# Layer 0 of a four-layer image network: the Fourier products in quarters of TensorE's array, and the w_out products written some rounds later

## The chip, the cores and the metric

The kernel runs on one core of a Trainium2 chip. The metric is the device time in microseconds of one execution. The engines are TensorE (PE: matmuls; PEld: its weight loads), VectorE (DVE), ScalarE (ACT), GpSimd (POOL) and SyncE (SP, which only issues DMAs here). TensorE's clock is granted by a throttle, and the profile shows what was granted (1.00 is full speed).

## What is computed

Four layers, each x = x + layer(group_norm(x)), on x of shape 4 x 48 x 256 x 256 in float32. Layers 1 and 2 scan over rows and columns, layer 3 is a relative of layer 0. The change is in layer 0:

```python
h = jnp.einsum('bchw,oc->bohw', x, w_in)            # 48 -> 192 channels
h = depthwise_3x3(h, w_dw)
x1, x2 = jnp.split(h, 2, axis=1)
h = gelu(x1) * x2                                   # 96 channels
y = jnp.einsum('bchw,oc->bohw', h, w_out)           # 96 -> 48 channels
yp = y cut into 8 x 8 patches
f = jnp.fft.rfft2(yp) * fft_w                       # a weight per channel and wave
y = jnp.fft.irfft2(f, s=(8, 8)), patches put together again
```

The transform of an 8 x 8 patch is a product with a fixed 64 x 64 matrix (64 real waves), and so is its inverse.

## The kernel before

**Tiling.** Layer 0 works on pairs of images: 2 x 48 channels on the partitions. A pair is cut into 32 strips of 8 rows, so there are 64 strips. Before layer 0, `input_stats` reads x once for the group norm; layer 0 gathers the statistics (`bn_stats`, L432) that the norm ahead of layer 1 needs, so layer 1 starts when the last strip is done.

**One strip.** The steps, with the functions and lines of the kernel before:

- `fetch` and `normed` (L234, ACT): load rows, scale and shift them.
- `hidden` (L256, PE, then a copy L259 on ACT) and `hidden_rest` (L264, PE, then two copies L268 on DVE): w_in. The hidden channels are split: 64 of each half go to tiles `main`, the other 32 to `rest`.
- `lane` (L285, PE): the 3x3 taps on `main`, as products with diagonal 32 x 32 weights on 16 tiles of the array. Two lanes, l = 0 and 1, each do nine taps per image, 8 products a tap; a "round" is one tap of both lanes, 16 products. At the end of an image lane 0 does the gelu (L296, ACT, tile `gl`) and lane 1 the product with it (L299, DVE, tile `g`).
- `unit` (L314 ACT, L320 DVE, 16 half-taps a strip; L328 to L330 ACT; L334 DVE): the 3x3 taps on `rest`, on VectorE, and their gate `gr`.
- `mixed` (L355 from `gr`, L362 from `g`, PE): w_out, into two PSUM tiles `py`, copied to `y` by ACT (L368).
- `turned` (L379, PE): 16 transposes, 8 into each of two PSUM tiles `pt`, each copied to `yt` by ACT (L383).
- `waves` (L393, PE): 4 products of the 128 x 128 matrix `dft` (two patches at once, block diagonal) with 448 columns; four VectorE products with the mask (L399) make `z`.
- `back` (L415, PE): 16 products, z as weights of 128 x 96, the permuted inverse as 128 columns; 16 VectorE sums with the residual `res` (L426), 4 statistics (L432), and a store issued by POOL (L435).

In the profile each float32 product is two TensorE passes (two LDWEIGHTS and two MATMUL records).

**Order.** For PE, DVE and ACT the order of instructions is that in which the program issues them. `in_turns` writes it: in each turn both lanes issue a tap, then the pieces of `work` (the steps above, with a cost each) as far as a credit goes that grows by `pace` a tap, then the half-taps of `unit` for VectorE. A piece has a condition; `mixed` waits until the strip's six parts are counted in `taken`. The pieces come one after the other: w_out of the strip before, then the halo, w_in `rest`, the transposes, w_in `main`, `waves`, `back`. Lane 1 begins four turns after lane 0.

**PSUM.** Layer 0 has four PSUM buffers of two banks (pool `ps0`, 4 buffers), shared by all of `ph`, `pd`, `py`, `pt`, `pf` and `po`. Each lane holds one for nine taps; it is free when the gelu (lane 0) or the product g (lane 1) has read it. So a new tile waits for the engine that reads the old one.

The loop that orders the pieces, as it stands before:

```python
if n:
    yield (
        lambda: taken.get(n - 1, 0) == 6, 4.0, lambda: state.update(y=mixed(n - 1)),
    )
...
if n:
    yield always, 3.3, lambda: state.update(z=waves(state["yt"])), 2.2
...
self.in_turns([lane(0), lane(1)], work(), 0.57, self.aside([unit(n) for n in range(len(strips))]))
```

Of the kernel before, what the change touches and what calls it, by code (L numbers as in the profile page):

```python
# [17 lines left out]
C = 48  # L18
CC = 2 * C
NT = 5  # L20
# [10 lines left out]
class Net:  # L31
# [9 lines left out]
    def __init__(self, ctx, tc, args, out, B, H, W):  # L41
# [20 lines left out]
        self.dft = self.load("dft", [128, 128])  # L62
# [3 lines left out]
        self.idft_p = self.load("idft_p", [128, 128])  # L66
# [10 lines left out]
    def new_stats(self, halves=False):  # L77


        n = self.B if halves else self.NP  # L80
        t = self.stat.tile([CC, n, self.NP * self.NCH // n, 6], F32, name=f"st{n}", tag="st")
        return [t[:, p] for p in range(n)]

    def norm(self, stats):

        nc, n = self.nc, len(stats)
        grp = self.grp if n == self.NP else self.grp6
        with self.tc.tile_pool(name="ps_n", bufs=1, space=PSUM) as psn:
            t = self.stat.tile([CC, 8, n], F32, name="nrm", tag=f"nrm{n}")
            mv = self.stat.tile([CC, n, 2], F32, name="mv", tag=f"mv{n}")  # L90
            sc = self.stat.tile([CC, n, 2], F32, name="sc", tag=f"sc{n}")
# [3 lines left out]
            pm = psn.tile([CC, n], F32, name="pm")  # L95
# [5 lines left out]
            pv = psn.tile([CC, n], F32, name="pv")  # L101
# [13 lines left out]
    def by_image(self, scs):  # L115

        found = []
        for p in range(self.NP):
            for b in range(2):
                t = self.stat.tile([CC, 2], F32, name=f"si{p}{b}", tag=f"si{p}{b}")  # L120
                for k in range(2):
                    self.nc.sync.dma_start(t[k * C : (k + 1) * C, :], scs[p][b * C : (b + 1) * C, :])
                found.append(t)
        return found
# [21 lines left out]
    def layer0(self, scs, stats):  # L146
# [7 lines left out]
        with ExitStack() as st:  # L154
# [42 lines left out]
            mask = wp.tile([128, 1, 1, C], F32, name="mask")  # L197
            nc.vector.tensor_copy(mask[:, 0, 0, :], pm[:, 0, 0, 0:C])
# [3 lines left out]
            raws, mains, rests, scp = [], [], [], []  # L202
            for k in range(2):
                raws.append(wp.tile([128, RB + 1, W], F32, name=f"raw{k}", tag=f"raw{k}"))
# [142 lines left out]
            def mixed(n):  # L347

                g, gr = state.pop((n, "g")), state.pop((n, "gr"))
                y = mid.tile([112, NQ, RB, PW], F32, name="y", tag="y", bufs=1)  # L350
# [15 lines left out]
                for k, py in enumerate(pys):  # L366
                    r = 2 * R2 * k
                    nc.scalar.copy(  # L368
                        y[:, :, r : r + 2 * R2, :].rearrange("p q r w -> p r q w"),
                        py[0:112].rearrange("p j r (q w) -> p (j r) q w", w=PW),  # L370
# [3 lines left out]
            def turned(y):  # L374
                yt = mid.tile([128, NQ, 112], F32, name="yt", tag="yt", bufs=1)
                for q0 in range(0, NQ, 8):
                    pt = ps.tile([128, 2, MM], F32, name="pt", tag="w")
                    for q in range(8):
                        nc.tensor.transpose(  # L379
                            pt[:, q // 4, q % 4 * 112 : (q % 4 + 1) * 112],  # L380
                            y[:, q0 + q].rearrange("p r w -> p (r w)"), self.ident[0:112, 0:112],
# [6 lines left out]
            def waves(yt):  # L388
                z = mid.tile([128, NQ, 2, C], F32, name="z", tag="z", bufs=1)
                for q0 in range(0, NQ, 8):  # L390
                    pf = ps.tile([128, 2, MM], F32, name="pf", tag="w")
                    for k in range(2):
                        nc.tensor.matmul(  # L393
                            pf[:, k, 0 : 4 * 112], self.dft,
                            yt[:, q0 + 4 * k : q0 + 4 * k + 4, :].rearrange("p q c -> p (q c)"),
                            start=True, stop=True,
                        )
                    for b in range(2):
                        nc.vector.tensor_tensor(  # L399
                            z[:, q0 : q0 + 8, b, :].rearrange("p (k q) c -> p k q c", k=2),  # L400
                            pf[:, :, 0 : 4 * 112].rearrange("p k (q c) -> p k q c", q=4)[:, :, :, 64 * b : 64 * b + C],
                            mask.to_broadcast([128, 2, 4, C]), ALU.mult,
                        )
                return z

            def back(n, z):

                p, h0 = strips[n]
                res = io.tile([CC, RB, W], F32, name="res")
                nc.sync.dma_start(res, self.x0[p, :, h0 : h0 + RB, :])  # L410
                xo = io.tile([CC, 2, self.WB, 2, RH, 2, 8], F32, name="xo")
# [933 lines left out]
```

## Time and profile before

| | |
|---|---|
| median of 3 runs | 14288.26 us (14286.5 to 14288.58) |
| the profiled execution's own time | 14286.4 us |
| its span, first to last instruction | 14284.6 us |
| mean granted TensorE clock over the span | 0.962 |
| busy: PE, DVE, ACT, POOL | 13196.5, 7393.2, 3661.9, 1340.3 us |
| layer 0, from the first to the 64th strip's w_out | 299.1 to 3277.7 us |
| PE busy, DVE busy, granted clock in that stretch | 2786.26, 2207.80 us, 0.94 |
| L415: busy, mean of a pass, passes | 239.1 us, 275 ns, 2048 |
| L393: busy, mean of a pass, passes | 210.7 us, 555 ns, 512 |
| L355: idle time ahead of it | 126.8 us, all of it ended by g (L299) |
| L379: idle time ahead of it | 56.6 us, of it 38.7 ended by ACT's gl and 15.8 by DVE's rest |

How to read it: a line of a group gives line, engine, operation, out<-in by the program's names, shapes and count, then busy time and mean duration of one, then the engine's idle time just ahead of them and what ended it. Passes on different tiles of the array overlap, so a mean duration is longer than the time that a pass adds. A line of the timeline gives start, duration, engine, line, operation and count, and in brackets the idle time ahead and what ended it. A line of stretches gives the stretch and its length, busy time and count of PE, PEld, DVE, ACT and POOL, then the granted clock, the DMA share and GB/s.

### The profile page before, as it was taken

Reading aid. Unit: us, or ns where it says so; the run is one execution under the profiler, and the core shown is the slowest. Engines: PE = TensorE matmul, PEld = TensorE weight load, DVE = VectorE, ACT = ScalarE, POOL = GpSimd, SP = SyncE. Lnnn points to the kernel's source line nnn. Section 1 sums busy time; section 2 is a strip of 40 time slices with the busy share of each in tenths; the row PEclk is TensorE's granted clock in tenths of the full one; section 3 lists DMA queues with packets and bytes.
Section 4 is the critical chain, followed back from the end, with each engine's and each line's share of the span. In section 5 each row is a group of like instructions: output and inputs, shape, how many; then the busy total and the mean of one; then the engine's idle time right before and its main releaser. Section 6 shows DMA issues by size and latency. Waiting matters only on the chain.

```text
span 14284.6 us, 338560 instructions
## 1 busy us (share of the span) xinstructions
PE 13196.5 (92%) x155716; PEld 8194.6 (57%) x155716; DVE 7393.2 (52%) x12064; ACT 3661.9 (26%) x3558; POOL 1340.3 (9%) x974
## 2 busy tenths in 40 slices
PE   2999999998999898889998988799999999999999
PEld 1444443446777676667776766555555555555555
DVE  6777777773333334443333344555555555455555
ACT  1333333332233000012230000133333333333333
POOL 0000010000000004410000044200000000000000
PEclk9999999999999999899999998899999999999999
DMA  7222222216755876777558767311111111111110
GB/s 166 49 54 48 55 51 52 50 48 119 152 139 153 161 146 166 179 146 151 135 160 159 154 149 192 75 24 20 24 20 24 20 24 20 20 24 20 21 23 18
DMA packets 1168858, 1219.07 MB, mean 85 GB/s; under 512 B 1026004, under 2 KB 1030604, under 8 KB 1106572
## 3 DMA queue, kind: packets, MB, share of 16 engines
q1 hardware_dynamic: 1069324, 649.62, 23.2%
q0 software_dynamic: 87488, 445.55, 11.2%
q10 hardware_dynamic: 10624, 102.24, 3.5%
q8 instruction: 1222, 20.02, 0.6%
q14 instruction: 200, 1.64, 0.0%
HBM read 699.84 MB, written 497.42 MB: 84 GB/s over the span
## 4 chain that ended last, share of the span: by engine, by line
PE 76%; DVE 10%; DMA 6%; ACT 3%; issue 2%; SPq 1%; POOL 1%; ACTq 0%; DVEq 0%; POOLq 0%
PE acc L609 33%; PE pd L1010 9%; PE pp L993 8%; PE pd L285 5%; PE pd L1026 4%; PE pz L964 4%; DMA blk<-x 3%; DVE acc L320 3%; PE po L1106 2%; PE pf L953 2%; PE ph L264 2%; PE ph L256 2%; DMA x<-blk 2%; PE py L355 1%; PE pf L393 1%
## 5 line engine op out<-in xcount | busy, mean ns | idle before, releaser
L609 PE MATMUL acc<-line,w_down 96*96 96x256 f32 x12240 | 2650.7, 379 | 42.5 <-DMA in<-x 23.5
L609 PEld LDWEIGHTS acc<-line,w_down 96*96 96x96 f32 x12240 | 1996.0, 163 | 696.6 <-issue 43.2
L1010 PE MATMUL pd<-z_a,diag 32*32 32x512 f32 x37152 | 1692.0, 596 | 2.7 <-ACT xt L943 0.7
L1070 DVE SCALAR_TENSOR_TENSOR acc<-z_b,wd,acc 128x1024 f32<-128x1024 f32 (+1 forms) x1056 | 1329.2, 1260 | 626.0 <-ACT acc L1067 595.4
L609 PE MATMUL acc<-line,w_left 96*96 96x256 f32 x6120 | 1362.3, 386 | 247.8 <-DVE line L792 247.8
L609 PE MATMUL acc<-line,w_right 96*96 96x256 f32 x6120 | 1338.0, 381 | 100.3 <-DVE line L753 36.2
L993 PEld LDWEIGHTS pp<-c_idft,z 128*128 128x128 f32 x10240 | 1185.0, 184 | 339.8 <-issue 195.4
L609 PEld LDWEIGHTS acc<-line,w_left 96*96 96x96 f32 x6120 | 1016.7, 166 | 593.1 <-DVE line L792 253.8
L285 PE MATMUL pd<-main,diag 32*32 32x512 f32 x36864 | 1338.4, 602 | 6.5 <-DVE g L299 6.4
L320 DVE SCALAR_TENSOR_TENSOR acc<-rest,wd,acc 128x1024 f32<-128x1024 f32 x1024 | 1326.7, 1341 | 1.9
L993 PE MATMUL pp<-c_idft,z 128*128 128x128 f32 x10240 | 1255.2, 282 | 65.6 <-DVE g_b L1037 39.0
L609 PEld LDWEIGHTS acc<-line,w_right 96*96 96x96 f32 x6120 | 1003.9, 164 | 434.5 <-DVE line L753 38.4
L1026 PE MATMUL pd<-z_b,diag 32*32 32x512 f32 x18432 | 1001.5, 602 | 59.2 <-DVE g_a L1053 39.6
L966 DVE TENSOR_TENSOR z<-pz,mask 128x512 f32<-128x512 f32 x1024 | 702.8, 686 | 519.1 <-PE pz L964 515.5
L753 DVE SCALAR_TENSOR_TENSOR line<-acc,b_right,in 96x256 f32<-96x256 f32 x1020 | 489.4, 480 | 880.6 <-PE acc L609 836.9
L285 PEld LDWEIGHTS pd<-main,diag 32*32 32x32 f32 x36864 | 525.8, 103 | 685.3 <-issue 514.4
L1010 PEld LDWEIGHTS pd<-z_a,diag 32*32 32x32 f32 x37152 | 601.6, 103 | 538.5 <-issue 358.8
L672 DVE TENSOR_TENSOR line<-acc,in 96x256 f32<-96x256 f32 x1020 | 429.1, 421 | 927.8 <-PE acc L609 913.3
L712 DVE SCALAR_TENSOR_TENSOR line<-acc,b_down,in 96x256 f32<-96x256 f32 x992 | 476.1, 480 | 808.5 <-PE acc L609 808.5
L104 ACT ACTIVATE nrm<-nrm 96x2 f32<-96x2 f32 (+1 forms) x4 | 0.8, 204 | 3333.5 <-DVE nrm L103 3333.5
L802 POOL TENSOR_TENSOR blk<-blk,line 96x1024 f32<-96x1024 f32 x248 | 705.7, 2874 | 863.5 <-DVE line L792 448.8
L792 DVE SCALAR_TENSOR_TENSOR line<-acc,b_left,in 96x256 f32<-96x256 f32 x992 | 475.7, 480 | 529.4 <-PE acc L609 529.4
(156 smaller groups left out, 12891.2 us busy)
## 6 DMA issues: line engine op xcount, KB each, us to landing
blk<-x ACTq DMA_DIRECT2D x64, 1536.0 KB, 23.3
in<-x SPq DMA_DIRECT2D x248, 384.0 KB, 11.1
dn<-line POOLq DMA_DIRECT2D x124, 768.0 KB, 9.6
rt<-line POOLq DMA_DIRECT2D x124, 768.0 KB, 10.0
in<-rt SPq DMA_DIRECT2D x124, 768.0 KB, 7.2
in<-dn SPq DMA_DIRECT2D x120, 768.0 KB, 7.2
in<-up SPq DMA_DIRECT2D x240, 384.0 KB, 11.1
up<-blk POOLq DMA_DIRECT2D x56, 1536.0 KB, 24.0
```

Of the source, the lines that this page charges most:

```text
L285: nc.tensor.matmul(pd[32 * j : 32 * j + 32, i], diag[s, t, :], z[s, R2 * j + t // 3 : R2 * j + t // 3 + R2, t % 3 : t % 3 + W], start=(t = ...
L320: nc.vector.scalar_tensor_tensor(to, at(t, r), wd[:, 1, t : t + 1], to, ALU.mult, ALU.add)
L609: self.nc.tensor.matmul(acc, w[:, t, :], carry[:, :, t : t + m], start=(t == 0), stop=(t == 2))
L712: nc.vector.scalar_tensor_tensor(inner(line), acc, bd, new[p][r], ALU.add, ALU.add)
L753: nc.vector.scalar_tensor_tensor(blocks(inner(line)), blocks(acc), br, new, ALU.add, ALU.add)
L802: (nc.vector if w0 == 0 else nc.gpsimd).tensor_tensor(part, part, inner(ln[p][:, f::2])[..., lo:hi].rearrange("p w i h -> p i h w"), ALU.add)
L964: nc.tensor.matmul(pz[:, b, 0 : 2 * HD], xf[s, q, :], wi[s, :], start=True, stop=True)
L966: nc.vector.tensor_tensor(z[:, q, 0 : 2 * n].rearrange("p (b c) -> p b c", b=2), pz[:, :, 0:n], mask[:, :, 0:n].to_broadcast([128, 2, n]), ...
L993: nc.tensor.matmul(pp[0:n, q // 4, :, q % 4 * PW : (q % 4 + 1) * PW], z[:, q0 + q, k * NM : k * NM + n], self.idft, start=True, stop=True,)
L1010: nc.tensor.matmul(pd[32 * j : 32 * j + 32, i, 0:n, :], diag[s, 2 if g == "m" else half, t, :], zt[g][s, R2 * j + t // 3 : R2 * j + t // 3 ...
L1026: nc.tensor.matmul(pd[to, i], diag[s, half, t, :], zt[f"b{half}"][s, R2 * j + t // 3 : R2 * j + t // 3 + R2, t % 3 : t % 3 + W], start=(t ...
L1070: nc.vector.scalar_tensor_tensor(made[0], at(t), wd[:, half, t : t + 1], made[0], ALU.mult, ALU.add)
```

## The change

- **Forward transform.** `dft` gives way to `fwd1`, the 64 x 64 matrix twice, one above the other. `y` is laid out so that the two patches of a transpose (index l) land on partitions 0 to 63 and 64 to 127 of `yt`. `waves` makes 8 products of 64 x 64 weights with 448 columns: row half by patch l, column half by the parity o of the patch column; the four (o, l) stand one after the other. Each l writes a PSUM bank of its own. The mask gets 112 columns (zeros between the images), so one VectorE product does what two did.
- **Inverse.** `idft_p` gives way to `inv1_p`. `back` makes 64 products: weights are 64 waves by 64 or 48 channels of z (image 0 on output partitions 0 to 63, image 1 from 64), moving 64 columns. Row half o writes bank o.
- **Images on partitions 0 and 64 on the way out.** `xo`, the residual (now two tiles `sums_of` that stay, loaded by two DMAs), the sums and the statistics have 112 partitions; the norm after layer 0 uses a matrix `grp7` of 112 x 112.
- **z** uses y's buffer.
- **w_out later.** The condition of `mixed` is now also that it has been asked four times (`gone`). The costs of `waves` and `back` go to 1.7 and 2.2, the pace to 0.52.

```diff
+                sums_of.append(wp.tile([CP, RB, W], F32, name=f"res{k}", tag=f"res{k}"))
+                nc.gpsimd.memset(sums_of[k][32:64], 0.0)
...
-                y = mid.tile([112, NQ, RB, PW], F32, name="y", tag="y", bufs=1)
+                y = mid.tile([CP, NQ, 2, RB, PW // 2], F32, name="y", tag="y", bufs=1)
...
-                z = mid.tile([128, NQ, 2, C], F32, name="z", tag="z", bufs=1)
+                z = mid.tile([128, NQ // 2, 2, CP], F32, name="z", tag="y", bufs=1)
                 for q0 in range(0, NQ, 8):
                     pf = ps.tile([128, 2, MM], F32, name="pf", tag="w")
-                    for k in range(2):
-                        nc.tensor.matmul(
-                            pf[:, k, 0 : 4 * 112], self.dft,
-                            yt[:, q0 + 4 * k : q0 + 4 * k + 4, :].rearrange("p q c -> p (q c)"),
-                            start=True, stop=True,
-                        )
-                    for b in range(2):
-                        nc.vector.tensor_tensor(
...
+                    for o in range(2):
+                        for l in range(2):
+                            f = slice(64 * l, 64 * l + 64)
+                            nc.tensor.matmul(
+                                pf[64 * o : 64 * o + 64, l, 0 : 4 * CP], self.fwd1[f, :], yt[f, q0 + o : q0 + 8 : 2, :],
+                                start=True, stop=True,
+                            )
+                    nc.vector.tensor_tensor(
+                        z[:, q0 // 2 : q0 // 2 + 4].rearrange("p q l c -> p l q c"),
+                        pf[:, :, 0 : 4 * CP].rearrange("p l (q c) -> p l q c", q=4),
+                        mask.to_broadcast([128, 2, 4, CP]), ALU.mult,
+                    )
...
-                res = io.tile([CC, RB, W], F32, name="res")
-                nc.sync.dma_start(res, self.x0[p, :, h0 : h0 + RB, :])
+                res = sums_of[n % 2]
+                for b in range(2):
+                    nc.sync.dma_start(res[64 * b : 64 * b + C], self.x0[p, b * C : (b + 1) * C, h0 : h0 + RB, :])
...
-                    po = ps.tile([128, 8, 2, 2, RH, 8], F32, name="po", tag="w")
-                    for q in range(8):
-                        nc.tensor.matmul(
-                            po[0:CC, q].rearrange("p e f h w -> p (e f h w)"),
-                            z[:, q0 + q].rearrange("p b c -> p (b c)"), self.idft_p,
-                            start=True, stop=True,
-                        )
+                    po = ps.tile([128, 2, 4, 2, 2, RH, 2, 4], F32, name="po", tag="w")
+                    for q in range(4):
+                        for l in range(2):
+                            for lo, m in ((0, 64), (64, C)):
+                                for o in range(2):
+                                    f = slice(64 * o, 64 * o + 64)
+                                    nc.tensor.matmul(
+                                        po[lo : lo + m, o, q, :, :, :, l, :].rearrange("p e f h w -> p (e f h) w"),
+                                        z[f, q0 // 2 + q, l, lo : lo + m], self.inv1_p[f, :],
+                                        start=True, stop=True,
+                                    )
...
+                asked = []
+
+                def gone():
+                    asked.append(0)
+                    return len(asked) % 4 == 0
+
...
-                            lambda: taken.get(n - 1, 0) == 6, 4.0, lambda: state.update(y=mixed(n - 1)),
+                            lambda: taken.get(n - 1, 0) == 6 and gone(), 4.0, lambda: state.update(y=mixed(n - 1)),
...
-                        yield always, 3.3, lambda: state.update(z=waves(state["yt"])), 2.2
+                        yield always, 1.7, lambda: state.update(z=waves(state["yt"])), 2.2
...
-                        yield always, 3.8, lambda: back(n - 1, state["z"]), 7.0
-
-            self.in_turns([lane(0), lane(1)], work(), 0.57, self.aside([unit(n) for n in range(len(strips))]))
+                        yield always, 2.2, lambda: back(n - 1, state["z"]), 7.0
+
+            self.in_turns([lane(0), lane(1)], work(), 0.52, self.aside([unit(n) for n in range(len(strips))]))
```

## The prediction

> **What bounds the kernel now.** I read the page's chain of work that ended last, then the busy times in chosen stretches, then PE's and VectorE's instructions in order of time over one strip of layer 0. The change touches layer 0 alone, so its lines come first:
>
> ```profile
> PE acc L609 33%; PE pd L1010 9%; PE pp L993 8%; PE pd L285 5%; PE pd L1026 4%; PE pz L964 4%; DMA blk<-x 3%; DVE acc L320 3%; PE po L1106 2%; PE pf L953 2%; PE ph L264 2%; PE ph L256 2%; DMA x<-blk 2%; PE py L355 1%; PE pf L393 1%
> ```
>
> L285, L320, L264, L256, L355 and L393 are layer 0, so it lies on the path, and the scans that follow need the statistics of all 64 strips: a microsecond saved there counts once. The first w_out product (L355) of the first strip starts at 299.1 us, that of the 64th at 3277.7: 63 strips in 2978.6 us, 47.28 each. Busy time by stretch (PE, PEld, DVE, ACT, POOL, then granted clock):
>
> ```profile
> 1117.22:1158.17 40.95, 38.10 (x666) 17.65 (x658) 31.40 (x45) 17.04 (x16) 4.44 (x4) 1.00 0.24 57
> 1158.17:1165.00 6.83, 6.44 (x38) 2.03 (x38) 3.92 (x4) 0.00 (x0) 0.00 (x0) 0.50 0.06 19
> 1165.00:1205.96 40.96, 38.18 (x674) 17.64 (x658) 31.33 (x45) 17.04 (x16) 4.45 (x4) 1.00 0.24 57
> ```
> ```profile
> 299.10:3277.70 2978.60, 2786.26 (x43737) 1230.01 (x43736) 2207.80 (x3018) 1064.43 (x1001) 282.31 (x252) 0.94 0.21 51
> ```
>
> Once a strip the clock is halved for 6.83 us. A mean of 0.94 means 0.06 / 0.5 = 12% of 2978.6 us at half speed, or 52 such stretches in 63 strips. From one to the next are 6.83 + 40.96 = 47.79 us, which is 7 x 6.83: the strip is locked to that grid. PE over the strip:
>
> ```profile
> 1155.11 1.12 PE L355 MATMUL py<-gr,wo_r 64*128 64x512 f32 x2
> 1158.56 3.78 PE L355 MATMUL py<-gr,wo_r 64*128 64x512 f32 x6 [2.33 <-DVE g L299]
> 1162.27 3.29 PE L362 MATMUL py<-g,wo 32*64 32x512 f32 x32
> 1165.49 2.35 PE L285 MATMUL pd<-main,diag 32*32 32x512 f32 x64
> ...
> 1175.32 0.98 PE L379 MATMUL pt<-c_ident,y 112*128 112x112 f32 x8 [0.31 <-DVE rest L268]
> 1176.91 0.99 PE L379 MATMUL pt<-c_ident,y 112*128 112x112 f32 x8 [0.60 <-ACT gl L296]
> ...
> 1187.29 3.27 PE L393 MATMUL pf<-yt,c_dft 128*128 128x448 f32 x8
> 1190.50 3.41 PE L285 MATMUL pd<-main,diag 32*32 32x512 f32 x96
> 1193.83 3.73 PE L415 MATMUL po<-c_idft_p,z 128*96 128x128 f32 x32
> 1197.50 5.54 PE L285 MATMUL pd<-main,diag 32*32 32x512 f32 x160
> ```
>
> PE stops 2.33 us for g (L299), and right after comes the half clock. And what VectorE does ahead of g:
>
> ```profile
> 1173.98 1.29 DVE L268 COPY rest<-ph 128x512 f32<-128x512 f32 x2 [0.52 <-PE ph L264]
> 1175.18 4.02 DVE L320 SCALAR_TENSOR_TENSOR acc<-rest,wd,acc 128x1024 f32<-128x1024 f32 x3
> ...
> 1196.33 3.25 DVE L426 TENSOR_TENSOR xo<-po,res 96x128 f32<-96x128 f32 x16
> 1199.49 2.46 DVE L432 BATCH_NORM_STATS2 st<-xo 96x6 f32<-96x512 f32 x4
> 1201.87 3.19 DVE L320 SCALAR_TENSOR_TENSOR acc<-rest,wd,acc 128x1024 f32<-128x1024 f32 x2
> 1204.99 1.21 DVE L299 TENSOR_TENSOR g<-gl,pd 128x1024 f32<-128x1024 f32 x1
> ```
>
> **Strip without the half clock.** From 1155.11 to the next py at 1202.97 (the timeline's next start) are 47.86 us. L355 from its restart to L285 took 1165.49 - 1158.56 = 6.93; the same work at full clock took 3.82 (2002.04 to 2005.86). So the half clock costs 3.11, and the strip would be 44.75 without it. Stalls in it: 3.45 from 1155.11 to 1158.56 less 0.49 for the pair itself (four pairs take 1.98 at 3277.68) = 2.96, and 0.91 at the transposes (L379).
>
> **What the Trainium skill says.** (1) "TensorE: Matmul & The Clock Gate", Part 1, puts the clock's activity window at 3413 ns and the clock at 4/8 or 8/8; its section "Why this matters for your kernels" wants no PE gap over about 3 us. The trace agrees on the two clocks and on 6.83 us = two windows, but 2.33 us of idle time was enough here; 0.66 us at 1862.94 was not (clock 1.00 from 1861.20 to 1902.00). (2) The same page's Part 1 gives about 25 ns from start to start of small matmuls. The trace starts 8 passes of L362 inside 0.065 us on eight tiles, so it is shorter here on separate tiles. (3) "TensorEngine Tiling (Array Packing)", Tiling Modes, names 64x64 with 4 independent tiles. No 64x64 product is in this trace; L362 (32x64) runs 8 at once: 32 passes in 1.92 us, where 4 in a row would need 4 x 0.43 by L393's rate. (4) "SBUF — State Buffer", Who interferes with whom: a VectorE instruction with two SBUF inputs blocks against a GpSimd one that reads SBUF. The trace agrees: the two taps at 1201.87 took 3.19, not 2 x 1.2, beside POOL's halo copy (1.05 us at 1201.73). g has one input in PSUM.
>
> **The change, part by part.**
>
> *pf in quarters.* Now 8 passes of 448 columns, 1190.50 - 1187.29 = 3.21 us: 0.376 each and 0.2 for the switch. After: 16 passes on four tiles at once, so 4 in a row: 1.5 + 0.2 = 1.70. Saves 1.5; at worst (two at a time) nothing.
>
> *po in quarters.* Now 32 passes of 128 columns in 3.67, 0.109 each and 0.18. After: 128 passes of 64 columns, 32 on each tile: 32 x 0.0545 + 0.2 = 1.95. Saves 1.72. That is the floor of its cost, as each quarter must stream its columns. The dear end: L285's 32 passes on 16 tiles take 1.09 us, 34 ns each, and 128 x 34 ns + 0.2 = 4.56, a loss of 0.9; by the page's 25 ns, 3.4. I take 1.95, because L362 shows starts far closer than either, and keep 4.56 for the range.
>
> *VectorE.* The mask product: 4 x 0.55 becomes 2 of 896 elements; between 384 (0.55) and 1024 (1.21) that is 1.08 each: nothing. The 16 sums and 4 statistics stay, on 112 partitions. VectorE is busy some 35 us of a strip and is the next bound.
>
> *At nothing.* y's copy with runs of 8 (ACT busy 17.04 of 41 us), the residual in two loads on SP (issued ahead, two buffers as before; no PE or VectorE wait on it shows), z in y's buffer (y is read by L379 and z by L415 long before each is written again), 112-row norm, memsets: ACT's, SP's and POOL's slack hides them. Without cover the residual's second load would cost about a microsecond a strip.
>
> *w_out later.* In the built program's order four rounds of 16 taps stand between g's issue and L355, where there was half a round (a round is 1.09 us). And g stands right after the statistics, ahead of the two taps (3.19) it now follows. From po's start at 0: sums 1.1 to 4.3, statistics to 6.7, g to 7.9. PE: po to 1.95, five rounds to 7.4, the first pair of L355 to 7.9. The stall of 2.96 falls to about 0.2 (bounds 0 and 2.96). ACT's copy of y and the transposes shift with it.
>
> *What is late next.* All later pieces move with L355. The image boundary (gelu, then g for the first image) now comes before the transposes. In the built order both transposes' buffers (four PSUM buffers in all) now wait for VectorE, where the second waited for ACT's gl; the three buffers that VectorE frees there are the two of L264 and the one that g frees, so one transpose waits for g. g stands behind L268 and three taps. On the clock of the strip above: VectorE starts L268 at 1173.98, taps 1175.18 to 1179.12, g to 1180.3. PE, from 1173.87: two rounds and eight transposes, ready for the second eight at 1176.95. New stall 3.35, replacing 0.91: +2.44. From strip 34 on the lanes run level instead of four rounds apart: the first eight wait for gl (0.9), the second for g (2.5), the same 3.4.
>
> *Sum.* 44.75 - 1.50 - 1.72 - 2.76 + 2.44 = 41.2 us a strip at full clock. But a 3.35 us pause is longer than the 2.33 us that halves the clock now, so I keep 3.1 for it: 44.3, close to the next step of the grid, 6.5 x 6.83 = 44.4. 63 x (47.28 - 44.3) = 188 us. The profiled execution took 14286.4 us (span 14284.6), so 14098; its runs' median is 1.9 above it: **14100**.
>
> **Rivals.**
> - *Half clock in part of the strips* (the pause straddles two windows, or my 3.1 us is too long): a mean of 42.8 gives 63 x 4.5 = 282, 14006. For it: 2.06 us at 2002.04 ran on at full clock. Against: 52 of 63 strips are caught now, by less.
> - *No half clock at all*: 41.2, 63 x 6.1 = 383, 13905. It needs the new pause under 2 us; the order speaks against that.
> - *Quarters bound by issue*: po at 3.4 to 4.56 puts the strip at 45.8 to 46.9: 14193 to 14264. For it: L285's 34 ns. Against: L362.
> - *Slower: two pauses, two half clocks.* If g still comes over 2 us after PE reaches L355 while the transposes pause too, the strip has 2.3 us more stall and another 3.1: 44.3 + 5.4 = 49.7, 63 x 2.4 = 153 us more, 14441. It decides from some 2 us of g's lateness at L355; my estimate leaves 1.8 us to that point.
>
> **Chances.** The forecast's case (14045 to 14170) 0.44; half clock in part (13950 to 14045) 0.20; none (13880 to 13950) 0.12; quarters dear (14170 to 14265) 0.13; about unchanged 0.03; slower 0.06; still faster 0.02. The range 13910 to 14260 leaves out some 0.18. A measurement of this kernel tells 0.2% (29 us) from no change; by that bound faster is 0.90, within it 0.04, slower 0.06.
>
> **What would show it.** L355's idle time on g falls from 126.8 us to under 30; L379's rises from 56.6 to some 150 to 210; a half-clock stretch a strip, now at the transposes, 44.4 us apart; po's group 2 us, pf's 1.7. I am wrong if the transposes don't wait for g, if po's group is over 3 us, or if the clock stays at 1.00 through layer 0.

## The result, and the profile after

The changed kernel takes 14251.55 us (median of 13 runs, 14221.72 to 14272.5) against 14292.23 for the kernel before on the same chips: a ratio of 0.9972, 95% interval 0.9963 to 0.998. It is faster by 41 us where 188 were forecast. The profiled execution took 14251.55 us, its span is 14249.7.

The busy times over layer 0, from the first strip's w_out to the 64th's (PE, PEld, DVE, ACT, POOL, then granted clock, DMA share, GB/s):

```profile
304.00:3223.00 2919.00, 2582.82 (x50194) 1048.63 (x50191) 2163.99 (x2889) 1072.77 (x1001) 274.39 (x252) 0.93 0.24 52
```

63 intervals of 46.33 us, where before had 47.28 and the forecast 44.3. The clock has not risen: 0.93, where it was 0.94. PE in order of time, over the strip that answers to the one shown of before:

```profile
1177.83 0.98 PE L386 MATMUL pt<-c_ident,y 112*128 112x112 f32 x8
1182.07 1.76 PE L386 MATMUL pt<-c_ident,y 112*128 112x112 f32 x8 [3.26 <-DVE g L306]
...
1193.93 1.73 PE L404 MATMUL pf<-yt,c_fwd 64*64 64x448 f32 x16
1195.59 2.35 PE L292 MATMUL pd<-main,diag 32*32 32x512 f32 x64
1197.87 2.08 PE L429 MATMUL po<-c_inv_p,z 64*64 64x64 f32 x128
1199.88 2.36 PE L292 MATMUL pd<-main,diag 32*32 32x512 f32 x65
1204.29 4.99 PE L292 MATMUL pd<-main,diag 32*32 32x512 f32 x95 [2.04 <-issue]
1209.21 1.99 PE L362 MATMUL py<-gr,wo_r 64*128 64x512 f32 x8
1211.13 1.97 PE L369 MATMUL py<-g,wo 32*64 32x512 f32 x32
```

Line by line: pf takes 1.73 us and po 2.08; the first product of w_out (L362) no longer waits; the second eight transposes wait 3.26 us for g. All this was forecast. Not forecast is the stop of 2.04 us in the middle of the taps (L292) behind po, put down to "issue", which is time in which PE waited for nothing that the profile shows. The clock was 0.50 from 1181.75 to 1185.16, behind the transposes' stop, and again from 1205.64 to 1209.05, behind the new one. What VectorE does ahead of g:

```profile
1175.66 1.29 DVE L275 COPY rest<-ph 128x512 f32<-128x512 f32 x2 [0.52 <-PE ph L271]
1176.86 4.02 DVE L327 SCALAR_TENSOR_TENSOR acc<-rest,wd,acc 128x1024 f32<-128x1024 f32 x3
1180.81 1.21 DVE L306 TENSOR_TENSOR g<-gl,pd 128x1024 f32<-128x1024 f32 x1
```

That is the order that the prediction read from the built program. The groups of PE over layer 0 (count, busy us and mean ns, then idle time ahead and its causes):

```profile
L292 PE MATMUL pd<-main,diag 32*32 32x512 f32 x36261 | 1498.5, 652 | 109.1 <-issue 103.8 <-DVE xo L440 4.9
...
L386 PE MATMUL pt<-c_ident,y 112*128 112x112 f32 x1024 | 155.4, 307 | 185.4 <-DVE g L306 168.8 <-ACT gl L303 14.5 <-ACT y L375 2.0
L429 PE MATMUL po<-c_inv_p,z 64*64 64x64 f32 (+1 forms) x8192 | 138.9, 219 | 35.8 <-issue 32.4 <-DVE g L306 2.6 <-DVE z L408 0.5
...
L362 PE MATMUL py<-gr,wo_r 64*128 64x512 f32 x512 | 133.5, 632 | 5.4 <-DVE gr L341 3.6 <-issue 1.8
```

The wait at w_out fell from 126.8 us to 5.4 and the transposes' rose from 56.6 to 185.4. New are 104 us at the taps and 32 at po put down to issue. Before, the taps' idle time was 6.5 us in all, and po's 1.5:

```profile
L285 PE MATMUL pd<-main,diag 32*32 32x512 f32 x36864 | 1338.4, 602 | 6.5 <-DVE g L299 6.4
...
L415 PE MATMUL po<-c_idft_p,z 128*96 128x128 f32 x2048 | 239.1, 275 | 1.5 <-issue 1.5
```

**What "issue" is here.** A queue of its own brings PE's instructions; the page of before, then that of after (packets, MB, share of the DMA engines):

```profile
q8 instruction: 1222, 20.02, 0.6%
```
```profile
q8 instruction: 1274, 20.87, 0.6%
```

The trace has 326129 instructions of PE (passes, weight loads, some semaphores): 256 for each of the 1274 packets, each of 16384 bytes. The Trainium skill, "Runtime: NRT & Kernel Launch", section "Instruction fetch mechanics", describes that: an engine's instruction memory is refilled in blocks of 256 instructions, by a DMA queue of the engine's own, and the cost of a block's boundary is called mostly hidden. The block agrees with the trace; "mostly hidden" does not hold here. I counted PE's instructions in order of time and took the number at which PE restarts after each stop over 0.2 us in layer 0 (a stop is counted here from 0.16 us ahead of the end that the profile models for the last pass, so it is that much longer than in the timeline). 80 stops, 152.6 us in all, restart at a number that leaves the remainder 193 when divided by 256 (below: 193 modulo 256), so all at the same place of a block. In the kernel before no place stands out: none, counting its neighbours, has more than 5 stops. Three of the 80, with the packet ahead of them (worked out from the trace's records):

```
PE stops  restarts  instruction  mod 256  packet starts  ends     restart after its end
1158.77   1159.94   30401        193      1156.84        1158.38  1.56
1202.09   1204.29   31937        193      1201.54        1203.04  1.25
1246.77   1250.36   33473        193      1247.58        1248.96  1.40
```

So PE has used up its block and waits for the next: in nearly all of these stops it restarts 1.2 to 1.6 us after a packet has ended. Below these stops are called pauses for instructions (restart within 1 of number 193: 81 of them, 154 us). po issues 256 instructions in 2.08 us (64 products, each with two weight loads and two passes), a whole block, while the taps take 2.35 us for 128.

And the packet is late. It starts at 1201.54, and in the microseconds ahead of it the DMA engines move the next strip's raw rows:

```
us from             1195  1196  1197  1198  1199  1200  1201  1202
KB of data in that     0    56   192   216   160   136     8     0
```

They were issued here, by SP, as soon as ScalarE's `normed` (1193.87 to 1195.97) had freed the buffer:

```profile
1195.99 0.78 SPq L232 DMA_DIRECT2D raw<-in_x  x2
```

Of 73 pauses over 0.3 us, 92% have more than 100 KB of data moved in the 4 us ahead of their packet (median 665 KB); of the other 320 packets 35% have. That is a coincidence in time so far; the experiments test it.

The records also show how far ahead a packet comes. Number the packets from the program's start by k. In layer 0 of the changed kernel no packet k starts before PE's instruction 256k + 147, and the pauses stand at 256k + 449: some 300 instructions are left when a packet can start at the earliest. From instruction 256k + 146 to the packet's start it takes 1.4 us (median) for the 213 packets with at most 100 KB of data in the 4 us ahead of them, and 3.9 us for the other 180; in the kernel before 1.2 and 3.6 us. With 1.05 us for the packet and 1.4 to the restart (medians), I estimate 3.9 us for a refill with no data in its way and 6.4 us behind data. In the kernel before, PE took at least 4.5 us for these 300 instructions; around po in quarters it takes as little as 2.5.

### The profile page after: what moved, and what is told of

The parts are those of the page before. It is cut to its first block, busy times and chain, and to the rows that moved or that the text cites. A ratio compares the mean times of both kernels' runs of the same rounds, so it can differ in the third digit from the quotient of the medians.

```text
span 14249.7 us, 351753 instructions
## 1 busy us (share of the span) xinstructions
PE 13004.8 (91%) x162372; PEld 8018.7 (56%) x162372; DVE 7354.4 (52%) x11937; ACT 3669.5 (26%) x3558; POOL 1333.9 (9%) x977
## 3 DMA queue, kind: packets, MB, share of 16 engines
q8 instruction: 1274, 20.87, 0.6%
## 4 chain that ended last, share of the span: by engine, by line
PE 81%; DMA 6%; DVE 6%; ACT 3%; issue 2%; POOL 1%; SPq 1%; ACTq 0%; DVEq 0%; POOLq 0%
PE acc L631 33%; PE pd L292 9%; PE pd L1032 9%; PE pp L1015 8%; PE pd L1048 4%; PE pz L986 4%; DMA blk<-x 3%; PE po L1128 2%; PE pf L975 2%; PE ph L271 2%; PE ph L263 2%; DMA x<-blk 1%; DVE acc L1092 1%; DMA gx<-in_x 1%; DVE acc L327 1%
## 5 line engine op out<-in xcount | busy, mean ns | idle before, releaser
L631 PE MATMUL acc<-line,w_down 96*96 96x256 f32 x12240 | 2650.8, 379 | 49.4 <-DMA in<-x 31.5
L292 PE MATMUL pd<-main,diag 32*32 32x512 f32 x36864 | 1524.7, 652 | 112.2 <-issue 103.8
L327 DVE SCALAR_TENSOR_TENSOR acc<-rest,wd,acc 128x1024 f32<-128x1024 f32 x1024 | 1279.0, 1299 | 2.0
L292 PEld LDWEIGHTS pd<-main,diag 32*32 32x32 f32 x36864 | 532.8, 107 | 922.0 <-issue 808.0
```

The costliest lines, as they stand in the source:

```text
L292: nc.tensor.matmul(pd[32 * j : 32 * j + 32, i], diag[s, t, :], z[s, R2 * j + t // 3 : R2 * j + t // 3 + R2, t % 3 : t % 3 + W], start=(t = ...
L327: nc.vector.scalar_tensor_tensor(to, at(t, r), wd[:, 1, t : t + 1], to, ALU.mult, ALU.add)
L631: self.nc.tensor.matmul(acc, w[:, t, :], carry[:, :, t : t + m], start=(t == 0), stop=(t == 2))
```

## The experiments

Theory 1: behind po PE runs out of fetched instructions, because 256 of them go in 2 us. It had rivals by number: an unnamed wait (2), the transposes' half clock alone (3), w_out later without gain (4), the order alone (5), VectorE as the bound (6), costs and pace without effect (7), the quarters held back by the transposes alone (8). Theory 9 came after e12: the refill's packet waits behind the load of the raw rows. In the table, "pauses" are those for instructions (restart within 1 of number 193 modulo 256), "pt idle" is the transposes' idle time, and "half" is the time at half clock (stretches that begin between the first and the 64th w_out), all in us over layer 0; "strip" is the mean of the 63 intervals. The expectations of e1 to e4 speak of 187 us in 94 pauses for the changed kernel, an earlier and wider count; by the one used here it has 154 us in 81.

| Kernel | time | ratio to before (95%) | strip | pauses | pt idle | half |
|---|---|---|---|---|---|---|
| before | 14292 | 1 | 47.28 | 5 | 57 | 386 |
| changed | 14252 | 0.9972 (0.9963-0.998) | 46.33 | 154 | 185 | 393 |
| e1 po on two row halves | 14109 | 0.987 (0.9856-0.9885) | 44.17 | 22 | 185 | 256 |
| e2 po in two pieces | 14179 | 0.992 (0.9905-0.9934) | 45.18 | 140 | 104 | 321 |
| e3 transposes apart, 1 round | 14125 | 0.9883 (0.9868-0.9897) | 44.27 | 149 | 122 | 215 |
| e4 po over all rows | 14098 | 0.986 (0.9843-0.9876) | 43.92 | 1 | 185 | 229 |
| e5 before, w_out later alone | 14064 | 0.9837 (0.982-0.9853) | 43.57 | 9 | 9 | 126 |
| e6 quarters alone | 14110 | 0.9873 (0.9858-0.9887) | 44.70 | 162 | 58 | 212 |
| e7 = e4, transposes 2 rounds apart | 13892 | 0.9717 (0.9703-0.9732) | 40.72 | 2 | 38 | 0 |
| e8 = e4, sixth asking | 14037 | 0.9817 (0.9802-0.9831) | 43.00 | 0 | 2 | 225 |
| e9 changed, old costs and pace | 14077 | 0.9852 (0.9837-0.9866) | 43.83 | 121 | 9 | 229 |
| e10 = e7, 64 extra products | 14113 | 0.9874 (0.9859-0.9889) | 44.19 | 52 | 38 | 89 |
| e11 = e2, transposes 2 apart | 13933 | 0.9751 (0.9735-0.9768) | 41.33 | 65 | 17 | 41 |
| e12 = e11, pieces further apart | 14035 | 0.9821 (0.9806-0.9835) | 42.97 | 70 | 3 | 154 |
| e13 changed, raw load moved | 14057 | 0.9835 (0.982-0.985) | 43.50 | 29 | 185 | 273 |
| e14 = e13, residual moved too | 14061 | 0.9836 (0.9821-0.9851) | 43.50 | 30 | 185 | 283 |
| e15 = e13, transposes 2 apart | 13847 | 0.9687 (0.9673-0.9702) | 40.12 | 10 | 38 | 14 |
| e16 = e14, transposes 2 apart | 13875 | 0.9708 (0.9692-0.9724) | 40.49 | 36 | 38 | 0 |
| e17 before, raw load moved | 14269 | 0.9983 (0.9976-0.9989) | 46.89 | 3 | 57 | 324 |
| e18 = e7, raw load moved | 13881 | 0.9717 (0.9701-0.9734) | 40.73 | 1 | 38 | 3 |

**e1: half the products.**
```diff
-for lo, m in ((0, 64), (64, C)):
-    for o in range(2):
-        matmul(po[lo : lo + m, o, q, ..., l, :], z[f, q0 // 2 + q, l, lo : lo + m], inv1_p[f, :])
+for o in range(2):
+    matmul(po[0:CP, o, q, ..., l, :], z[f, q0 // 2 + q, l, :], inv1_p[f, :])
```


> The changed kernel with one edit: po in 32 products of all 112 columns on two row halves, in place of 64 products on four quarters; the same numbers and the same streamed columns for each row half (32 passes of 64 columns, about 1.95 us), but 64 weight loads and 64 passes a strip instead of 128 and 128. Theory 1 (PE runs out of fetched instructions after po): the pauses put down to issue in layer 0, 187 us over 94 pauses in the changed kernel, fall below 90 us, po stays near 2 us, and the time falls from 14252 to 14060-14160. Theory 2 (the pauses are a wait for a buffer or a semaphore that the profile doesn't name): po is as long as before and nothing else moves, so the pauses stay at 150 us or more and the time at 14230-14270.

Pauses 22 us and time 14109, as theory 1 had it. But po took 3.36 us, not 2: two things changed, the count and the pace, so this alone doesn't separate them.

**e2: the same products in two pieces.** `back` is called twice, for q0 = 0 and 8, with one round of taps between.


> The changed kernel with one edit: the 64 products of po stay as they are, but are issued in two pieces of 32 with one round of 16 taps between. The number of instructions is unchanged, and so is PE's work. Theory 1 (fetched instructions run out): 128 instructions in 1 us, then 32 or more at the taps' pace, then 128 again: the pauses fall by a third to a half, from 187 to 90-130 us, and the time to 14150-14220. Theory 2 (an unnamed wait): pauses at 150 us or more, time 14230-14290, the sums of the second half being about 1 us later.

The time is as expected of theory 1, the pauses are not: 140 us, 14 less. With the 73 us went 82 us of the transposes' wait, which fell to 104, and 72 us of half clock; why that wait fell I did not follow. So e2 does not tell the theories apart.

**e3: the transposes in two pieces.**
```diff
-yield always, 1.8, lambda: state.update(yt=turned(state["y"]))
+yield always, 0.9, lambda: turned(state["y"], 0)
+yield always, 0.9, lambda: turned(state["y"], 1)
```


> The changed kernel with one edit: the second eight transposes are issued one round of 16 taps (1.1 us) after the first eight. Theory 1: the pauses after po stay (150 us or more of 187), the transposes' idle time falls from 185 to some 110-130 us, time 14150-14210. Theory 3 (the gain was lost to the half clock that the transposes' 3.3 us pause sets off, and to nothing else): with a pause of 2.2 us the half clock stays in most strips or goes in many; if it goes, the time falls to 14000-14080.

126 us gained, more than expected: pt idle 122 and 178 us less of half clock, with pauses as before (149). The transposes' wait is thus one loss, and the pauses, which stayed, are another.

**e4: po over all rows.** One product of 128 x 112 weights and a block-diagonal second factor of 128 columns takes the place of four.


> The changed kernel with one edit: po in 16 products over all 128 rows with a block-diagonal second factor of 128 columns, as long as in the kernel before (about 3.7 us), 32 weight loads and 32 passes a strip. pf stays in quarters and w_out late. Theory 1: the pauses put down to issue almost vanish (under 30 us of 187), which pays for the 1.6 us a strip (100 us) that po takes longer: 14080-14180. Theory 2: the pauses stay, and the longer po is added: 14320-14370.

Pauses 1 us. po takes 3.75 us again, 1.67 more than in quarters, and the kernel is 154 us faster than the changed one all the same. The idle time at the taps is gone:

```profile
L292 PE MATMUL pd<-main,diag 32*32 32x512 f32 x36432 | 1421.7, 631 | 0.7 <-issue 0.6
...
L426 PE MATMUL po<-c_inv_p,z 128*112 128x128 f32 x2048 | 240.4, 276 | 1.4 <-DVE g L306 0.9 <-DVE z L408 0.5
```

**e5 and e6: each part alone.**


> The kernel before with one part of the change alone: w_out is written at every fourth asking. Products, their costs and the pace are those of before. In the built order the first image's g now stands half a round behind both groups of transposes, so they needn't wait for it. Theory 1 (PE runs out of fetched instructions only behind po's 128 products; before's 32 passes don't do that): L355's idle time falls from 127 us to under 30, no pauses put down to issue (under 20 us), the strip goes from 47.3 to 42-44 us and the time to 13960-14120. Theory 4 (w_out later gains nothing, since g is as late relative to PE wherever it stands): L355's or the transposes' idle time stays at 150 us or more, the time within 0.3% of before.

> The changed kernel with w_out written as in the kernel before (at the first asking; pace 0.57 as before); both Fourier products stay in quarters. VectorE's sums after po, statistics and g set when w_out can start, and po is shorter by 1.6 us, so PE reaches w_out earlier and waits longer there: idle time at w_out 3.0 + 1.6 = 4.6 us a strip, some 290 us, of which the pauses for instructions hide a part. Theory 1: pauses for instructions stay (100-190 us) but cost little beside that wait; pf's 1.5 us a strip remain as the gain: 14150-14290. Theory 5 (the quarters gain what was forecast, 3.2 us a strip, and only their place behind w_out loses it): 14030-14100.

w_out later alone gains 232 us, the quarters alone 186, both together 41. e5's wait at w_out and at the transposes, then e6's at the input projection and at the transposes:

```profile
L355 PE MATMUL py<-gr,wo_r 64*128 64x512 f32 x512 | 167.3, 632 | 14.2 <-DVE g L299 7.4 <-DVE gr L334 5.5
...
L379 PE MATMUL pt<-c_ident,y 112*128 112x112 f32 x1024 | 115.5, 265 | 9.2 <-DVE rest L268 7.1 <-ACT y L368 2.0
```
```profile
L263 PE MATMUL ph<-xn,wi 48*128 48x512 f32 (+1 forms) x996 | 270.7, 642 | 74.5 <-DVE g L306 74.5
...
L386 PE MATMUL pt<-c_ident,y 112*128 112x112 f32 x1024 | 126.8, 268 | 57.6 <-ACT gl L303 37.1 <-DVE rest L275 18.4 <-ACT y L375 2.0
```

In e5 neither of the two losses is there, and the intervals are mostly 41.1 us up to the 30th; from there they are up to 53 us long, and from the 34th strip on the lanes run level and the input projection waits for ScalarE's gelu. In e6 the pauses are there in full (162 us), but not the wait of 290 us at w_out that I expected: PE is idle there for 16 us, and waits 75 us for g at the input projection. That PE, held up by its own pauses, arrives later at w_out fits this, but was not tested. e6 lies in neither range: theory 1's lower end was 40 us too long, theory 5's upper end 10 us too short. Theory 4 falls with e5.

**e7 and e8: e4 without the transposes' wait.** e7 is e4 with `turned` in two pieces at costs 1.9 and 0.9; e8 is e4 with `% 6` for `% 4`.


> The changed kernel with two edits: po in 16 products over all rows (32 passes, 3.7 us), and the second eight transposes two rounds of 16 taps after the first eight. Theory 1 with its second part (what is lost is the pauses for instructions, the transposes' wait for g, and the half clock that either sets off): idle time at the transposes under 60 us instead of 185, pauses for instructions under 30 us, half clock under 100 us in place of 393, strip 39-41 us, time 13780-13920. Theory 6 (VectorE is the bound of the strip, so that removed waits come back elsewhere): new waits for VectorE at py, pf or ph of over 100 us, time 13980-14080.

> The changed kernel with two edits: po in 16 products over all rows, and w_out at every sixth asking instead of every fourth. Up to the 34th strip the first image's g then stands three rounds ahead of the transposes and the second image's g ahead of po; from the 34th on the g follows the transposes and stands ahead of the input projection's products. Theory 1: transposes' idle time under 60 us, half clock under 150 us, time 13800-13980. Theory 6 (VectorE is the bound): waits of over 100 us at other lines, time 14000-14100.

e7 over its layer 0, in the same columns as above:

```profile
303.70:2869.20 2565.50, 2511.94 (x44145) 1100.19 (x44142) 2163.74 (x2887) 1068.88 (x1001) 342.94 (x252) 1.00 0.27 59
```

The clock is 1.00 and PE is busy 98% of the time: with the pauses gone and the transposes' wait down to 38 us, no half clock is left. e8 missed theory 1's range: the transposes' wait went (2 us), but waits of 67 and 69 us came up at the taps and the input projection:

```profile
L292 PE MATMUL pd<-main,diag 32*32 32x512 f32 x36258 | 1388.5, 623 | 66.9 <-ACT y L375 33.2 <-DVE z L408 23.9 <-ACT main L266 9.7
L263 PE MATMUL ph<-xn,wi 48*128 48x512 f32 (+1 forms) x996 | 292.3, 707 | 68.9 <-ACT gl L303 68.2
```

In time and size that is what theory 6 had forecast. Its cause is not: 24 of these 136 us wait for VectorE, 111 for ScalarE, and in e7 VectorE does the same work in strips of 40.7 us. The sum of the waits decides, not the one that was aimed at.

**e9: only the plan's numbers undone.**
```diff
-yield always, 1.7, ... waves     yield always, 2.2, ... back     pace 0.52
+yield always, 3.3, ... waves     yield always, 3.8, ... back     pace 0.57
```


> The changed kernel with one edit in the plan alone: the costs of the two Fourier steps and the pace as in the kernel before (3.3, 3.8, 0.57 in place of 1.7, 2.2, 0.52). Both products stay in quarters and w_out late; the order is then that of the run with w_out later alone (14064), with both groups of transposes ahead of the first image's g. Theory 1 (what was lost is the pauses for instructions behind po, the transposes' wait for g, and the half clock): transposes' idle time under 30 us instead of 185, pauses for instructions still 120-200 us; against w_out later alone 63 x 3.1 = 195 us gained by the quarters and some 150 lost to the pauses, with more half clock: 14000-14100. Theory 7 (the new costs and pace matter nothing): 14230-14270, transposes at 150 us or more.

```profile
L386 PE MATMUL pt<-c_ident,y 112*128 112x112 f32 x1024 | 114.1, 263 | 9.2 <-DVE rest L275 7.1 <-ACT y L375 2.0
```

Pt idle 9 us, and 175 us faster than the changed kernel: w_out's later place and the quarters do not put the transposes behind g unless the new costs and pace come with them. Whether costs and pace would do it with w_out early is open: e6 has the new costs, but the old pace, and its transposes wait as in the kernel before. Pauses are still 121 us, and e9 (14077) is no faster than e5 (14064), which has neither product in quarters.

**e10: the instructions by themselves.** e7 with 64 small products a strip ahead of po's.


> The best kernel so far (po over all rows, the transposes two rounds apart; 13892, pauses for instructions 3 us, no half clock) with 64 extra products a strip, of four columns each on the four quarters, ahead of po's own products, which then write over them: the results are unchanged, and PE has 128 more weight loads and 128 more passes a strip, as many instructions as po in quarters has. Their own time is some 1 to 1.7 us a strip (63 to 107 us). Theory 1 (PE runs out of fetched instructions where many come in a short time): pauses of 100-200 us in layer 0 at one place modulo 256 of PE's instruction count, half clock again, time 14060-14260. Theory 2 (an unnamed wait of the po in quarters itself): no pauses, only the products' time: 13950-14000.

The pauses are back, at the same number 193 modulo 256 (34 of 36), with half clock, in a kernel whose po is as in e7. They are a quarter to a half of what I expected (52 us). The extra products themselves took more than expected, 2.2 us a strip: from po's first start to its last it is 5.72 us, in e7 3.48.

**e11 and e12: quarters, spread out.**


> The changed kernel with po's 64 products on the quarters issued in two pieces a round apart, and the second eight transposes two rounds after the first eight. Against the best kernel so far (13892) po is 1.7 us a strip shorter (105 us) and has 192 more instructions. Theory 1: pauses for instructions of 100-150 us in layer 0 and some half clock: 13900-14050, not faster than 13892. Theory 8 (without the transposes' wait the quarters pay): 13780-13850.

> As the run before it, but po's two pieces stand further apart, on either side of the last input projection's products (which issue 16 instructions in 2 us), so that no 256 instructions follow each other in under about 4.5 us at that place. Theory 1: pauses for instructions under 60 us; if g's new place ahead of the input projection costs no new wait, 13780-13880; with a wait of 1 us a strip there, 13850-13950. Theory 2: pauses unchanged at 100-150 us.

e11 came out as theory 1 had it in time, with fewer pauses (65); e12 missed on both counts: pauses 70, and 66 us of waits at the input projection, which now stands behind z. Nor did it spread the instructions as meant: the fastest 256 of a strip take 2.8 us (median over the strips), where 4.5 was meant, e11 has 3.3, e2 2.6 and the changed kernel 1.8. What the three share with the changed kernel is the raw load at its old place: 66 of e2's 70 pauses, 45 of e11's 50 and all 48 of e12's have more than 100 KB of data in the 4 us ahead of their packet.

**e13 and e14: the same instructions, other places for the loads.**
```diff
-nc.sync.dma_start(raw[...])        # at the head of the strip's steps
+nc.scalar.dma_start(raw[...])      # behind the copies in turned
```


> The changed kernel with one edit: the load of the next strip's raw rows is issued on ScalarE's queue, in order behind the copies of the transposes (some 20 us ahead of po, where no other transfer runs), instead of on SP, where it starts just ahead of po. PE's instructions and their order are unchanged. Theory 9 (the refill of PE's instructions waits behind that load while po uses them up fast): pauses for instructions fall from 154 us to under 70, half clock with them, time 14080-14180. Theory 1 alone (256 instructions in 2 us are too many, whatever is transferred): pauses 130-170 us, time 14230-14270.

> As the run before it, and the load of the residual rows, which SP issues just behind po, moves to the same place. Theory 9: the second kind of pause (some 10 us behind po, 30 or so in the changed kernel) goes too: pauses under 40 us, time 14050-14150. Theory 1 alone: as the changed kernel, 14230-14270.

In e13 PE's products and their order are those of the changed kernel. The load now stands 15 us ahead of po, and behind po:

```profile
1165.21 0.79 ACTq L232 DMA_DIRECT2D raw<-in_x  x2
```
```profile
1179.96 2.08 PE L433 MATMUL po<-c_inv_p,z 64*64 64x64 f32 x128
1181.97 1.15 PE L296 MATMUL pd<-main,diag 32*32 32x512 f32 x31
1183.68 4.73 PE L296 MATMUL pd<-main,diag 32*32 32x512 f32 x129 [0.55 <-issue]
```
```profile
L296 PE MATMUL pd<-main,diag 32*32 32x512 f32 x36463 | 1454.5, 635 | 17.7 <-issue 12.4 <-DVE xo L444 5.0
...
L390 PE MATMUL pt<-c_ident,y 112*128 112x112 f32 x1024 | 151.7, 302 | 185.3 <-DVE g L310 168.7 <-ACT gl L307 14.5 <-ACT y L379 2.0
```

The packets start at 1181.03 and 1184.92, in quick succession, and the pauses fall from 154 us to 29. The transposes' wait is unchanged to 0.1 us, and the kernel is 195 us faster than the changed one. 125 us of that are the pauses, and 60 would be the half clock (120 us less of it, at half the work). Moving the residual's load as well (e14) gave nothing. So the count of theory 1 is one half of the cause, and the load in the refill's way (theory 9) the other. Of the 36 pauses that are left in e13, 30 have no such data ahead: there PE uses up its 300 instructions in 3.2 us (median), less than the 3.9 us estimated for a refill.

**e15 and e16: the quarters with both waits removed.**


> The changed kernel with two edits: the second eight transposes two rounds after the first eight, and the load of the raw rows moved as before; po stays in 64 products on quarters. Against po over all rows with the same transposes (13892) po is 1.67 us a strip shorter, 105 us. Theory 9: pauses under 60 us, no half clock or little, 13790-13870. Theory 1 alone: pauses of 100 us and more and some half clock, 13920-14020.

> As the run before it, with the load of the residual moved as well. Theory 9: pauses under 30 us, no half clock: 13770-13830. Theory 1 alone: 13920-14020.

e15 is the fastest version, 13847 us, 3.1% faster than before and 2.8% than the changed kernel:

```profile
298.50:2826.00 2527.50, 2447.99 (x50197) 1009.15 (x50190) 2156.05 (x2888) 1070.00 (x1001) 343.02 (x252) 1.00 0.27 60
```
```profile
L435 PE MATMUL po<-c_inv_p,z 64*64 64x64 f32 (+1 forms) x8192 | 137.4, 219 | 6.9 <-issue 5.2 <-DVE g L310 1.2 <-DVE z L414 0.5
```

po costs 137 us where e7's costs 240, and PE has 7 us of idle time there. e16 is 29 us slower than e15 with pauses of 36 us again; it missed its range by 45 us. Its trace shows why: the two loads are issued together on ScalarE's queue, 1536 KB at once. Of the 48 pauses 23 come with a packet right behind that data, and 22 of the other 25 with one that starts within 4.5 us of the packet before it, which had mostly been held up itself.

**e17 and e18: the load's move by itself.**


> The kernel before with the raw rows' load moved to ScalarE's queue behind the copies of the transposes, nothing else. Theory 9 (the load costs only where it holds up a refill that PE needs at once): no change beyond 0.3%, 14250-14330. If the load's place is worth something by itself (ScalarE's input earlier, less contention): 14100-14200, and then the gain of the same move in the changed kernel was not the refill alone.

> The kernel with po over all rows and the transposes two rounds apart (13892), with the raw rows' load moved in the same way. Theory 9: no change beyond 0.2%, 13865-13920, so that the 46 us by which the quarters with the moved load (13847) are faster come from po. If the load's place is worth something by itself: 13700-13850.

24 us in the kernel before, nothing in e7 (the same ratio), 195 in the changed kernel: the move gains most where many instructions follow each other next to it, and some 24 of the 195 may have another reason. Against e18 the quarters of e15 bring 34 us, not po's whole 103: over layer 0 the taps are busy 52 us longer (1379.5 for 1327.5) and PE waits 20 us longer at them (33.7 for 13.9), 19 of it for VectorE's sums after po. Why they are busy longer no run shows.

## Why the prediction was wrong

By its own steps:

- *pf and po in quarters.* Right: 1.73 for 1.70, 2.08 for 1.95. The rival "bound by issue" (3.4 to 4.56 us) is out by its own mark, though the measured time lies in its range: the group is as short as the forecast had it, and the time is lost behind it.
- *The wait at w_out.* Right: 126.8 us to 5.4.
- *"What is late next".* Right in cause, place and size: the second transposes wait for g, 3.26 us for 3.35. What set that order I gave as the later place of w_out; e9 shows that this alone doesn't do it, and that the new costs and pace are needed.
- *Half clock, 3.1 us a strip.* Right in size, by two faults that cancel. I kept one stretch of 6.83 us a strip, 44.4 apart. There are 82 in 63 strips, of 3.41 and 6.83, behind two kinds of stop; 393 us of it cost 393 / 2 / 63 = 3.1 a strip. That the size came out is luck: with most pauses gone and the transposes' wait as it was (e13), 273 us are left, or 2.2 a strip. The lock to a grid is gone: strips around the one shown vary from 44 to 54 us.
- *The sum.* 46.33 - 3.1 of half clock - 154 / 63 = 2.45 of pauses leaves 40.8 at full clock, where I had 41.2. The terms that I wrote down hold, and e13, with most of the pauses gone, takes 14057 where 14100 was forecast. The step that failed is "po in quarters": "I take 1.95", as the time of its passes, with the number of instructions not priced. It had no term for the supply of 192 more of them a strip; measured in its place are 154 us of pauses, 2.45 us a strip, and the half clock behind them. Nor do the columns alone set the pace of the quarters, as I wrote: e10's products of 4 columns follow each other on a tile as slowly (58 ns) as these of 64. It failed together with "At nothing": it went through SP's residual load, but not SP's raw load, which stood beside po already and cost little while po had 64 instructions (pauses 5 us; e17 gains 24 us by moving it).
- *The account.* In the profiled runs the span fell by 34.9 us. The 63 intervals gave 59.6, of 188 forecast: 154 short of it for the pauses, 25 ahead for the strip. Against it stand 4.9 at layer 0's start (the first w_out comes between 295.5 and 311.9 us over all runs, so this is scatter), 10.4 from the 64th w_out to the first scan product, and 9.5 in the scans and layer 3, which I did not follow. Of the 10.4, 8 are a longer wait for layer 1's first load (31.5 us of idle time for 23.5).

What stays open: where a packet waits while data moves. That it queues behind the load in the DMA engines is what e13 and the 1.4 and 3.9 us fit; that queue itself no record shows.

## What to carry to other kernels

When a change cuts products into smaller ones, price the instructions as well as the passes: count weight loads and passes over the shortest stretch, and look at what the DMA engines move at that moment. Idle time "for issue" whose restarts share one instruction number modulo 256 was a wait for the refill here, and shifting a load took most of it away (154 us to 29) without touching PE's work. And run each part of a change alone: here each part was worth 186 us or more, and together they were worth 41.

## What the runs showed of the hardware that I had not expected

- No two packets of PE's instructions start within 3.3 us of each other in the changed kernel's layer 0 (3.6 in before's), while po uses 256 in 2.08 us. A packet itself takes 0.9 to 2.0 us (median 1.05), and PE mostly restarts 1.2 to 1.6 us after it.
- From pass to pass on one tile it took 58 ns (median) with 64 x 64 weights and 64 columns (the changed po), the same 58 with 4 columns (e10), 98 with 64 x 112 weights and 64 columns (e1), and 109 with 128 x 112 and 128 columns (e4). By pf of before (0.376 us for 448 columns) 64 columns alone are 54 ns and 128 are 107. So in e10 and e1 something other than the columns sets the pace. A weight load of some 0.9 ns a weight column beside the pass, the longer of the two deciding, fits all four; that is an estimate, and no run tests it. The two row halves of e1 do run side by side, but at 98 ns a pass.
- A stop of some 2 us was mostly followed by half clock: in layer 0 of the kernel before, a stretch at 0.50 began during the stop or within 6.83 us of the restart for 49 of the 51 stops of 2.0 to 2.5 us, and for none of the 60 stops of 0.5 to 1 us. e7's regular 0.98 us at the transposes never had one.
